# Turning Wk at the sixth tile, summing two biases on GpSimd, and spreading the reading of the expert weights

## The chip, the cores and the metric

The kernel runs on one core of a Trainium2 chip. The metric is the device time of one execution in microseconds. A core has a matrix engine (TensorE, "PE" in the profile, its weight loads "PEld"), three engines for elementwise work (VectorE "DVE", ScalarE "ACT", GpSimd "POOL"), a queue processor (SyncE, "SP") and 16 DMA engines. The engines run side by side, each works off its own list in order, and they wait for one another through semaphores.

## What is computed

A layer-normalised input of 2 x 1024 tokens of width 512 goes through attention (one head of width 512) and, beside it, through a mixture of 8 experts of which each token uses two. The second result gates the first:

```python
x = L0_attn_hidden_states
xn = _layernorm(x, axis=-1)
s = _L0_attn_ref(xn, w_qkv, b_qkv, w_out, b_out)
g = _silu(_L0_ffn_ref(xn, router_w, router_b, expert_w, expert_b, proj_w, proj_b, norm_w))
x = x + s * g
```

In attention `q, k, v = split(xn @ w_qkv.T + b_qkv)`, the scores are `q @ k.T / sqrt(512)`, softmax over keys, then `context @ w_out.T + b_out`. In the experts part, the logits `xn @ router_w + router_b` choose two experts with softmax weights; each expert is `silu(xn @ expert_w[e] + expert_b[e])`; the mix is projected, added to `xn`, and RMS-normalised.

## The kernel before

Everything is float32. The tokens are 16 tiles of 128 (`NT`), eight for each batch.

**Folded weights.** The kernel does not form q, k and v. It multiplies Wv with Wout once (`product_vo`, into `rwvo`), so that a tile's value rows come out of one product already in output form, and Wq with Wk (`product`, into `wqk`). Biases are folded too. `weighted(w_, bias, name)` forms a sum over four 128-row pieces of a weight, each multiplied by a column of bias: one multiplication, then three multiply-and-adds, four VectorE operations of 128 x 512. `columns` then sums over partitions with four one-column products against `ones`. Three such sums exist. `sq` (from Wq and bk) gives one extra router column `pw` that is stored in `rw[:, :, E]`, so that every tile's product over `rwvo` needs it. `sk` (from Wk and bq) gives `pu`, copied into `u`, the bias of the queries. `vb` (from Wout and bv) is summed over partitions by the product `pvb` and added to the output bias `bo`.

**Turned weights.** `wZ[0]` (Wq) and `wZ[1]` (Wk) come in by DMA and are transposed by `turn_w`: four VectorE transpositions of 128 x 512 into `wqkT`. All four must be done before any 128-row piece of `wqkT` is whole.

**The head.** GpSimd's list starts with constants and its share of the loads. VectorE takes statistics (`parts`), `means` and `variances` finish them with one small product each (`pmean`, `pvar`), ScalarE takes the root with `ln_eps` as its bias and normalises (`norm`), VectorE transposes the tile (`turn_x`), and SP writes the normalised tile to DRAM (`store`). Tiles 0 and 1 are done ahead of the loop.

**The tile loop** (line 500), t = 2 to 15. Step t transposes tile t+1 on VectorE, multiplies tile t by `rwvo` on TensorE (`value_half`, two halves with four products each, into `pv`), copies tile t-1 out of PSUM on ScalarE (`keep_values`) and normalises tile t+2. Statistics are closed for four tiles at a time, at t = 2, 5 and 9, by `means` between the halves and `variances` after them. Single pieces of other work hang on chosen steps: the turning of Wk at t = 8, `sk` at 9, `vb` at 10, `pu` at 11, `pvb` at 12, and the reads of all expert weights at 13 (32 DMAs of 256 KB, half issued by SP and half by GpSimd).

**After the loop** come the routing on VectorE, beside the products `pqk` and `pq`, then 39 expert slots (gather by GpSimd, two passes through DRAM for a transposition, four products of 512 columns each), then attention and the final gate.

**Order.** `keep_order` makes each engine keep the order in which the source issues its work. Temporary memory comes from pools: the `raw` pool holds the incoming weights and the three sums. The expert weights' tile `ew` takes that memory after `close(raw_guard)`, so its reads wait until the last readers of `raw` are done.

Of the kernel before, what the change touches and what calls it, by code (L numbers as in the profile page):

```python
# [10 lines left out]
FP = mybir.dt.float32  # L11
# [3 lines left out]
ALU = mybir.AluOpType  # L15
# [5 lines left out]
P = 128  # L21
LN_EPS = 1e-5
RMS_EPS = 1e-6
# [4 lines left out]
def kernel(  # L28
# [17 lines left out]
    B, S, H = hidden.shape  # L46
    E = router_w.shape[1]
    KC = H // P
# [13 lines left out]
    const = ctx.enter_context(tc.tile_pool(name="const", bufs=1))  # L62
    keep = ctx.enter_context(tc.tile_pool(name="keep", bufs=1))
    dram = ctx.enter_context(tc.tile_pool(name="dram", bufs=1, space=DRAM))
    ps_mm = ctx.enter_context(tc.tile_pool(name="ps_mm", bufs=4, space=PSUM))

    def pool(name, bufs=1, side="left", **where):
        guard = tc.tile_pool(name=name, bufs=bufs, side=side, reuse_waits="tile", **where)
        return guard, guard.__enter__()
# [3 lines left out]
    def close(guard):  # L73
        guard.__exit__(None, None, None)
# [25 lines left out]
    pe, dve, act, gps, sp = nc.tensor, nc.vector, nc.scalar, nc.gpsimd, nc.sync  # L100
# [8 lines left out]
    QP = P // 4  # L109
# [16 lines left out]
    def spread(eng, z, rows, quarters=range(4)):  # L126
        for q in quarters:
            eng.dma_start(
                z[ts(q, QP)], rows[:, ts(q, P)].rearrange("(i a) f -> a i f", a=QP)
            )  # L130

    def turn_w(dst, z):

        for r in range(KC):
            dve.transpose(
                dst.rearrange("p j (i q a) -> p i j q a", i=4, q=4)[:, :, :, r, :],
                z[:, ts(r, 4), :].rearrange("p i (j b) -> p i j b", b=QP),
            )
# [18 lines left out]
    wqkT = qT.rearrange("p k c f -> p (k c f)").rearrange("p (n f) -> p n f", f=H)  # L157
# [3 lines left out]
    raw_guard, raw = pool("raw", side="right")  # L161
# [6 lines left out]
    rw = rwvo[:, :, HH : HH + E1]  # L168
# [5 lines left out]
    def load_x(eng, quarters, t, n):  # L174
        for q in quarters:
            eng.dma_start(
                x[ts(q, QP), ds(t, n)].rearrange("p t i f -> p (t i) f"),
                xr_d[ds(t * P, n * P), ts(q, P)].rearrange("(n a) f -> a n f", a=QP),
            )

    wv_in = raw.tile([P, KC, H], FP, name="wv_in")
    wZ = [raw.tile([P, H // QP, P], FP, tag=f"wZ{i}", name=f"wZ{i}") for i in range(2)]
    wo = raw.tile([P, KC, H], FP, name="wo")
    bqkv = const.tile([P, 3, KC], FP, name="bqkv")
    bqk = const.tile([P, 2, KC], FP, name="bqk")
# [14 lines left out]
    ours, others = (0, 1), (2, 3)  # L200
# [28 lines left out]
    for q in range(4):  # L229
        for j in range(KC):  # L230
            gps.tensor_copy(bqk[ts(q, QP), :, j], bqkv[ts(j, QP), 0:2, q])  # L231
    spread(gps, wZ[0], w_qkvT[:, ts(0, H)], others)
    load_x(gps, others, 2, 2)
    for q in range(4):
# [1 line left out]
            rw[ts(q, QP), :, 0:E], router_w[ts(q, P), :].rearrange("(j b) e -> b j e", b=QP)  # L236
        )
    load_x(gps, others, 4, 4)
    ln_eps = const.tile([P, 1], FP, name="ln_eps")
    gps.memset(ln_eps, LN_EPS)  # L240
    rms_eps = const.tile([P, 1], FP, name="rms_eps")
    gps.memset(rms_eps, RMS_EPS)
    order = rc.tile([P, E], FP, name="order")
    for e in range(E):
        gps.memset(order[:, e : e + 1], float(E - e))
    ones = const.tile([P, P], FP, name="ones")
    gps.memset(ones, 1.0)

    rb = const.tile([P, E1], FP, name="rb")
    gps.dma_start(rb[:, 0:E], router_b.partition_broadcast(P))  # L250
    bo = const.tile([P, H], FP, name="bo")
# [15 lines left out]
    u = const.tile([P, KC], FP, name="u")  # L267
# [49 lines left out]

    def weighted(w_, bias, name):  # L320

        s_ = raw.tile([P, H], FP, tag="s", name=name, bufs=3)
        for c in range(KC):
            b_ = bias[:, c : c + 1]
            if c:
                dve.scalar_tensor_tensor(s_, w_[:, c, :], b_, s_, ALU.mult, ALU.add)
            else:
                dve.tensor_scalar(s_, w_[:, c, :], b_, None, ALU.mult)
            yield s_

    def columns(s_, name):

        ps = ps_mm.tile([P, 512], FP, tag="mm", name=name)
        for c in range(KC):
            pe.matmul(
                ps[:, c : c + 1], lhsT=s_[:, ts(c, P)], rhs=ones[:, 0:1], start=True, stop=True
            )
        return ps[:, 0:KC]

    def parts(t):  # L340
        for i in range(4):
            dve.bn_stats(st[:, t, i].rearrange("p h k -> p (h k)"), x[:, t, i, :])

    def across(a, name):

        ps = ps_mm.tile([P, 512], FP, tag="mm", name=name)
        n = a.shape[1] * 2
        pe.matmul(
            ps[:, :n], lhsT=eighth, rhs=a.rearrange("p m h -> p (m h)"), start=True, stop=True
        )  # L350
        return ps[:, :n].rearrange("p (m h) -> p m h", h=2)

    def means(t, n):
        g_ = ds(4 * t, 4 * n)
        at_ = st.rearrange("p t i h k -> p (t i) h k")[:, g_]
        dve.tensor_reduce(mean[:, g_], across(at_[:, :, :, 1], f"pmean{t}"), AX.X, ALU.add)
        dve.tensor_tensor(
            dev[:, g_],
            at_[:, :, :, 1],
            mean[:, g_].unsqueeze(2).to_broadcast([P, 4 * n, 2]),  # L360
            ALU.subtract,
        )
        dve.tensor_tensor(dev[:, g_], dev[:, g_], dev[:, g_], ALU.mult)
        dve.scalar_tensor_tensor(
            dev[:, g_], at_[:, :, :, 2], 8.0 / H, dev[:, g_], ALU.mult, ALU.add
        )
# [26 lines left out]
    def turn_x(t):  # L393
        turn(xnT[t // ST][:, :, ts(t % ST, P)], x[:, t], "(i a)")
# [49 lines left out]
    bb = raw.tile([P, KC], FP, name="bb")  # L444
# [2 lines left out]
    parts(2)  # L447
    parts(3)
    product_vo(1, 3)
    sum_q = weighted(wqkT[:, 0:KC], bqk[:, 1], "sq")  # L450
    next(sum_q)
    next(sum_q)


    pvs = {}
# [1 line left out]
    def value_half(t, n):  # L457
        if t not in pvs:
            pvs[t] = ps_big.tile([P, 2, 512], FP, tag="big", name=f"pv{t}")
        cols = (ds(0, HH + E1), ds(HH + E1, HH))[n]  # L460
        for c in range(KC):
            pe.matmul(  # L462
                pvs[t][:, n, : HH + E1 * (1 - n)],
                lhsT=xnT[t // ST][:, c, ts(t % ST, P)],
                rhs=rwvo[:, c, cols],
                start=(c == 0),
                stop=(c == KC - 1),
            )
# [5 lines left out]
        act.copy(lg1[:, t, :], pv[:, 0, HH : HH + E1])  # L474

    value_half(0, 1)
    means(2, 2)
    next(sum_q)
    sq_ = next(sum_q)
    value_half(1, 1)  # L480
    variances(2, 2)
    norm(2)
    norm(3)
    pbb = ps_mm.tile([P, 512], FP, tag="mm", name="pbb")
    pe.matmul(pbb[:, 0:KC], lhsT=ones, rhs=bb, start=True, stop=True)
    dve.tensor_reduce(rb[:, E:E1], pbb[:, 0:KC], AX.X, ALU.add)
    dve.tensor_copy(rw[:, :, E], columns(sq_, "pw"))
    value_half(0, 0)
    turn_x(2)
    keep_values(0)  # L490
# [9 lines left out]
    for t in range(2, NT):  # L500
        if 2 < t < NT - 1:
            turn_x(t + 1)
        value_half(t, 1)
        keep_values(t - 1)
        if t in (2, 5, 9):
            first = {2: 4, 5: 8, 9: 12}[t]
            means(first, 4)
        value_half(t, 0)
        if t in (2, 5, 9):
            variances(first, 4)  # L510
        if t + 2 < NT:
            norm(t + 2)
            if t % 2:
                store(t + 1)
        if 3 <= t < 7:
            parts(2 * t + 2)
            parts(2 * t + 3)
        if t == 2:
            gps.dma_start(bo, b_out.partition_broadcast(P))
        if t == 8:  # L520
            turn_w(wqkT[:, KC:], wZ[1])
        if t == 9:
            *_, sk_ = weighted(wqkT[:, KC:], bqk[:, 0], "sk")
        if t == 10:

            *_, vb = weighted(wo, bqkv[:, 2], "vb")
        if t == 11:
            dve.tensor_copy(u, columns(sk_, "pu"))
        if t == 12:
            pvb = ps_mm.tile([P, 512], FP, tag="mm", name="pvb")  # L530
            pe.matmul(pvb, lhsT=ones, rhs=vb, start=True, stop=True)  # L531
            dve.tensor_tensor(bo, pvb, bo, ALU.add)
            close(raw_guard)
        if t == 13:
            ew_guard, ewp = pool("ew", side="right")
            ew = ewp.tile([P, E, KC, H], FP, name="ew")
            for e in range(E):
                for q in range(4):
                    (sp if q in ours else gps).dma_start(  # L539
                        ew[ts(q, QP), e],  # L540
                        expert_w[e, ts(q, P), :].rearrange("(j b) f -> b j f", b=QP),
                    )
    keep_values(NT - 1)
    dve.tensor_tensor(lg1, lg1, rb.unsqueeze(1).to_broadcast([P, NT, E1]), ALU.add)
    close(ln_guard)
# [107 lines left out]
    first = rt.tile([P, E], FP, name="first")  # L653
# [48 lines left out]
    for g in range(2 * NT // LG):  # L702
# [7 lines left out]
        for j in range(LG):  # L710
# [3 lines left out]
                lhsT=lsel[:, j, :],  # L714
                rhs=tsel[:, i].rearrange("p k s -> p (k s)"),
                start=(i == 0),
                stop=(i == 2 * NT - 1),
# [40 lines left out]
    pw = pwp.tile([P, KC, H], FP, name="pw")  # L758
# [604 lines left out]
```

## Time and profile before

| what | value |
|---|---|
| three runs | 538.69, 541.28, 543.67 us; median 541.28 |
| the profiled execution | 540.82 us, its span 539.1 us |
| mean granted clock of TensorE | 0.995 |
| DMA | 112.37 MB, 208 GB/s over the span |
| VectorE's `sk`, its first operation and the three others | start 68.21 us, 0.48 and 2.33 us |
| VectorE's `vb`, the same | start 71.59 us, 0.44 and 2.33 us |
| GpSimd between its read of `bo` and its first read of `ew` | idle for 51.17 us |
| first and last issue of `ew` by SP, then `eb` | from 84.72 us, over 26.03 us; 111.78 us |

A row of the timeline gives a start in microseconds, a duration, engine, line and operation, the tile written and the tiles read; in brackets stands how long the engine was idle before it and what ended that. A row of groups gives the busy sum in us, the mean of one in ns, and the idle time before. Float32 products appear as two records each, so four products make eight. The digits of the slices are tenths of the busy share in 40 equal pieces of the span. A row of windows gives the stretch, its length, busy time with the number of instructions, the granted clock of TensorE, the DMA share and the bandwidth.

### The profile page before, as it was taken

To read this page: it belongs to the slowest core of one execution; us is meant where nothing else is said; L and a number is where in the kernel's file an instruction comes from. 1 tells how busy PE (TensorE), PEld (TensorE's weight loads), DVE (VectorE), ACT (ScalarE), POOL (GpSimd) and SP (SyncE) were. 2 spreads that over 40 slices of the span, in tenths; PEclk is the share of its full clock that TensorE was granted. 3 is DMA by queue.
4 is the path that set the end of the run, shared out by engine and by line. 5 is a ranking of instruction groups with operands and counts; after the bars stand their busy time and mean duration, and the time that the engine had idled before them with its cause. 6 is when DMAs were issued, how large, how long until landed. Compare 5 with 4: busy or idle time off the path is not lost.

```text
span 539.1 us, 5950 instructions
## 1 busy us (share of the span) xinstructions
PE 527.3 (98%) x1762; PEld 322.1 (60%) x1762; DVE 311.2 (58%) x565; ACT 167.0 (31%) x316; POOL 236.0 (44%) x272
## 2 busy tenths in 40 slices
PE   7999999999999999999999999999999999999996
PEld 5778877444444444444466656756846657484585
DVE  2565652840333333333859376375697685949586
ACT  1535562211311111111333422423426234152340
POOL 8610006022234875230227445246189755464542
PEclk9989999999999999999999999999999999999999
DMA  9995339999999999994387922723625638295512
GB/s 212 206 220 127 78 79 227 275 217 336 319 338 331 359 348 338 318 290 146 125 281 234 299 83 92 273 78 123 229 78 179 230 95 297 71 312 176 187 54 78
DMA packets 89057, 112.37 MB, mean 208 GB/s; under 512 B 6849, under 2 KB 59201, under 8 KB 88897
## 3 DMA queue, kind: packets, MB, share of 16 engines
q1 hardware_dynamic: 75072, 75.51, 47.5%
q0 software_dynamic: 8192, 26.24, 16.4%
q10 hardware_dynamic: 5760, 10.23, 5.0%
q8 instruction: 15, 0.25, 0.2%
q14 instruction: 18, 0.14, 0.1%
HBM read 70.54 MB, written 41.42 MB: 208 GB/s over the span
## 4 chain that ended last, share of the span: by engine, by line
PE 87%; DVE 6%; issue 3%; DMA 2%; POOL 1%; ACT 1%; DVEq 0%; POOLq 0%
PE ph L814 20%; PE so L1147 17%; PE pp L1076 14%; PE po L1013 10%; PE pv L462 10%; PE pq L555 5%; PE pr L574 4%; PE sc L1057 3%; PE pqk L586 3%; DMA wZ<-in_L_attn_w_qkv_dram 2%; DVE sc L1082 1%; DVE pT L120 1%; ACT x L380 1%; POOL bqk L231 1%; DVE h L840 1%
## 5 line engine op out<-in xcount | busy, mean ns | idle before, releaser
L814 PE MATMUL ph<-ew,gT 128*128 x280 | 120.3, 592 | 0.0
L814 PEld LDWEIGHTS ph<-ew,gT 128*128 128x128 f32 x280 | 53.2, 190 | 66.9 <-issue 66.9
L788 POOL DMA_INDIRECT xg<-xn_d,tok x39 | 37.3, 957 | 78.2 <-DMA xs<-xg 52.2
L840 DVE TENSOR_TENSOR h<-ph,eb 128x512 f32<-128x512 f32 x39 | 26.8, 690 | 75.6 <-issue 40.4
L462 PE MATMUL pv<-rwvo,xnT 128*128 128x256 f32 (+1 forms) x256 | 60.9, 394 | 1.8 <-DVE xnT L120 1.0
L462 PEld LDWEIGHTS pv<-rwvo,xnT 128*128 128x128 f32 x256 | 48.6, 194 | 11.2 <-ACT x L380 1.4
L843 ACT ACTIVATE h<-h 128x512 f32<-128x512 f32 x39 | 24.5, 629 | 97.7 <-DVE h L840 89.0
L1013 PE MATMUL po<-pw,ct 128*128 128x512 f32 x112 | 49.2, 592 | 0.0
L975 POOL DMA_INDIRECT hg<-ho_d,posi_m x32 | 32.4, 1013 | 37.0 <-DVE nm L1041 23.4
L1044 ACT ACTIVATE pr<-sc,nm 128x1024 f32<-128x1024 f32 x16 | 18.3, 1145 | 90.7 <-DVE nm L1041 89.0
L1154 DVE TENSOR_TENSOR o<-so,o 128x256 f32<-128x256 f32 x49 | 20.0, 421 | 38.8 <-PE so L1147 25.9
L1192 POOL TENSOR_TENSOR o<-o,base 128x512 f32<-128x512 f32 x14 | 20.6, 1493 | 45.3 <-DVE o L1157 45.3
L1076 PE MATMUL pp<-xnT,qT 128*128 128x512 f32 x84 | 39.5, 592 | 0.0
L1147 PE MATMUL so<-vo,pT 128*128 128x256 f32 x168 | 38.5, 379 | 0.0
L1013 PEld LDWEIGHTS po<-pw,ct 128*128 128x128 f32 x112 | 21.3, 190 | 25.5 <-issue 25.3
L1147 PEld LDWEIGHTS so<-vo,pT 128*128 128x128 f32 x168 | 31.9, 190 | 7.3 <-issue 2.6
L120 DVE STREAM_TRANSPOSE gT<-sz 128x512 f32<-128x512 f32 x39 | 27.4, 702 | 13.4 <-DMA sz<-xs 13.4
L1082 DVE TENSOR_TENSOR sc<-pp,sc 128x512 f32<-128x512 f32 x49 | 31.6, 679 | 5.2 <-PE pp L1076 5.2
L539 POOL DMA_DIRECT2D ew<-in_L_ffn_expert_w_dram x16 | 8.7, 551 | 57.6 <-PE pvb L531 51.2
L574 PE MATMUL pr<-xnT,wqk 128*128 128x256 f32 x128 | 28.8, 381 | 0.9 <-DVE sc L1082 0.9
L120 DVE STREAM_TRANSPOSE pT<-pz 128x1024 f32<-128x1024 f32 x14 | 28.2, 2011 | 0.2 <-DMA pz<-ps 0.2
L574 PEld LDWEIGHTS pr<-xnT,wqk 128*128 128x128 f32 x128 | 24.2, 190 | 6.6 <-DVE sc L1082 2.2
(227 smaller groups left out, 819.9 us busy)
## 6 DMA issues: line engine op xcount, KB each, us to landing
xs<-xg SPq DMA_DIRECT2D x39, 256.0 KB, 4.7
sz<-xs SPq DMA_DIRECT2D x39, 256.0 KB, 4.6
ho_d<-h ACTq DMA_DIRECT2D x39, 256.0 KB, 4.7
ps<-pr SPq DMA_DIRECT2D x16, 512.0 KB, 3.3
pz<-ps SPq DMA_DIRECT2D x16, 512.0 KB, 5.7
xn_d<-x SPq DMA_DIRECT2D x32, 128.0 KB, 2.4
ew<-in_L_ffn_expert_w_dram POOLq DMA_DIRECT2D x16, 256.0 KB, 10.9
ew<-in_L_ffn_expert_w_dram SPq DMA_DIRECT2D x16, 256.0 KB, 13.6
```

What stands on the lines that cost most here:

```text
L120: dve.transpose(dst.rearrange(f"p j {order} -> p i j a", a=QP), z.rearrange("p i (j b) -> p i j b", b=QP),)
L462: pe.matmul(pvs[t][:, n, : HH + E1 * (1 - n)], lhsT=xnT[t // ST][:, c, ts(t % ST, P)], rhs=rwvo[:, c, cols], start=(c == 0), stop=(c == KC ...
L555: pe.matmul(ps[:, half, :], lhsT=wqk[:, c, ts(oc, P)], rhs=xnT[0][:, c, ts(half, 512)], start=(c == 0), stop=(c == KC - 1),)
L574: pe.matmul(ps[:, :PW], lhsT=wqk[:, c, ts(oc, P)], rhs=xnT[1][:, c, ts(k, PW)], start=(c == 0), stop=(c == KC - 1),)
L788: gps.indirect_dma_start(out=xg[s], out_offset=None, in_=xn_d, in_offset=bass.IndirectOffsetOnAxis(ap=tok[:, s : s + 1], axis=0),)
L814: pe.matmul(ph, lhsT=g_[:, c, :], rhs=ew[:, ds(r, 1), c, :].rearrange("p e f -> p (e f)"), start=(c == 0), stop=(c == KC - 1),)
L840: dve.tensor_tensor(h, ph, eb[:, ds(r, 1), :].rearrange("p e f -> p (e f)"), ALU.add)
L975: gps.indirect_dma_start(out=g_, out_offset=None, in_=ho_d, in_offset=bass.IndirectOffsetOnAxis(ap=posi_m[:, n, t : t + 1], axis=0),)
L1013: pe.matmul(po, lhsT=c_[:, c, :], rhs=pw[:, c, :], start=(c == 0), stop=(c == KC - 1))
L1076: pe.matmul(ps, lhsT=l_[:, c, :], rhs=r_[:, c, :], start=(c == 0), stop=(c == KH - 1))
L1082: dve.tensor_tensor(dst, ps, other, ALU.add)
L1147: pe.matmul(ps[:, :w_], lhsT=l_[:, c, :], rhs=r_[:, c, :], start=(c == 0), stop=(c == SK - 1),)
```

## The change

`ln_eps`, `rms_eps` and `ones` are filled by GpSimd ahead of its first weight load. `weighted` takes an engine. On VectorE it does what it did; on another engine, each multiply-and-add is a multiplication into a temporary `m_` (two of these exist) and an addition, seven operations in all. `sq` stays on VectorE but is done in one go ahead of the value products of tiles 0 and 1; the second half of tile 1, `means`, `pbb` and `pw` are reordered around it, and `pw` is copied before `variances`. `vb` goes to GpSimd at t = 2 and `pvb` to t = 4. Wk is turned at t = 5, `sk` follows on GpSimd, `pu` is at t = 8, where `raw` is closed. The reads of the experts go one expert a step, t = 8 to 15. The statistics of tiles 12 to 15 move from t = 5 and 6 to t = 6 and 7.

```diff
+    ln_eps = const.tile([P, 1], FP, name="ln_eps")
+    gps.memset(ln_eps, LN_EPS)
+    rms_eps = const.tile([P, 1], FP, name="rms_eps")
+    gps.memset(rms_eps, RMS_EPS)
+    ones = const.tile([P, P], FP, name="ones")
+    gps.memset(ones, 1.0)
     spread(gps, wZ[0], w_qkvT[:, ts(0, H)], others)
...
     load_x(gps, others, 4, 4)
-    ln_eps = const.tile([P, 1], FP, name="ln_eps")
-    gps.memset(ln_eps, LN_EPS)
-    rms_eps = const.tile([P, 1], FP, name="rms_eps")
-    gps.memset(rms_eps, RMS_EPS)
...
-    ones = const.tile([P, P], FP, name="ones")
-    gps.memset(ones, 1.0)
...
-    def weighted(w_, bias, name):
+    def weighted(w_, bias, name, eng):
         s_ = raw.tile([P, H], FP, tag="s", name=name, bufs=3)
         for c in range(KC):
             b_ = bias[:, c : c + 1]
             if c:
-                dve.scalar_tensor_tensor(s_, w_[:, c, :], b_, s_, ALU.mult, ALU.add)
+                if eng is dve:
+                    dve.scalar_tensor_tensor(s_, w_[:, c, :], b_, s_, ALU.mult, ALU.add)
+                else:
+                    m_ = raw.tile([P, H], FP, tag="m", name=f"{name}_m{c}", bufs=2)
+                    eng.tensor_scalar(m_, w_[:, c, :], b_, None, ALU.mult)
+                    eng.tensor_tensor(s_, s_, m_, ALU.add)
             else:
-                dve.tensor_scalar(s_, w_[:, c, :], b_, None, ALU.mult)
-            yield s_
+                eng.tensor_scalar(s_, w_[:, c, :], b_, None, ALU.mult)
+        return s_
...
-    sum_q = weighted(wqkT[:, 0:KC], bqk[:, 1], "sq")
-    next(sum_q)
-    next(sum_q)
+    sq_ = weighted(wqkT[:, 0:KC], bqk[:, 1], "sq", dve)
...
     value_half(0, 1)
+    value_half(1, 1)
     means(2, 2)
-    next(sum_q)
-    sq_ = next(sum_q)
-    value_half(1, 1)
+    pbb = ps_mm.tile([P, 512], FP, tag="mm", name="pbb")
+    pe.matmul(pbb[:, 0:KC], lhsT=ones, rhs=bb, start=True, stop=True)
+    dve.tensor_copy(rw[:, :, E], columns(sq_, "pw"))
     variances(2, 2)
     norm(2)
     norm(3)
-    pbb = ps_mm.tile([P, 512], FP, tag="mm", name="pbb")
-    pe.matmul(pbb[:, 0:KC], lhsT=ones, rhs=bb, start=True, stop=True)
     dve.tensor_reduce(rb[:, E:E1], pbb[:, 0:KC], AX.X, ALU.add)
-    dve.tensor_copy(rw[:, :, E], columns(sq_, "pw"))
...
-        if 3 <= t < 7:
-            parts(2 * t + 2)
-            parts(2 * t + 3)
+        if t in (3, 4, 6, 7):
+            first = {3: 8, 4: 10, 6: 12, 7: 14}[t]
+            parts(first)
+            parts(first + 1)
         if t == 2:
             gps.dma_start(bo, b_out.partition_broadcast(P))
-        if t == 8:
-            turn_w(wqkT[:, KC:], wZ[1])
-        if t == 9:
-            *_, sk_ = weighted(wqkT[:, KC:], bqk[:, 0], "sk")
-        if t == 10:
-            *_, vb = weighted(wo, bqkv[:, 2], "vb")
-        if t == 11:
-            dve.tensor_copy(u, columns(sk_, "pu"))
-        if t == 12:
+            vb = weighted(wo, bqkv[:, 2], "vb", gps)
+        if t == 4:
             pvb = ps_mm.tile([P, 512], FP, tag="mm", name="pvb")
             pe.matmul(pvb, lhsT=ones, rhs=vb, start=True, stop=True)
             dve.tensor_tensor(bo, pvb, bo, ALU.add)
+        if t == 5:
+            turn_w(wqkT[:, KC:], wZ[1])
+            sk_ = weighted(wqkT[:, KC:], bqk[:, 0], "sk", gps)
+        if t == 8:
+            dve.tensor_copy(u, columns(sk_, "pu"))
             close(raw_guard)
-        if t == 13:
             ew_guard, ewp = pool("ew", side="right")
             ew = ewp.tile([P, E, KC, H], FP, name="ew")
-            for e in range(E):
-                for q in range(4):
-                    (sp if q in ours else gps).dma_start(
...
+        if 0 <= t - 8 < E:
+            e = t - 8
+            for q in range(4):
+                (sp if q in ours else gps).dma_start(
```

More of the change, by code (lines that the diff above doesn't have):

```diff
@@ L532 @@
             dve.tensor_tensor(bo, pvb, bo, ALU.add)
+        if t == 5:
[3 more added lines that the diff above has]
+            dve.tensor_copy(u, columns(sk_, "pu"))
             close(raw_guard)
-        if t == 13:
             ew_guard, ewp = pool("ew", side="right")
             ew = ewp.tile([P, E, KC, H], FP, name="ew")
-            for e in range(E):
-                for q in range(4):
-                    (sp if q in ours else gps).dma_start(
-                        ew[ts(q, QP), e],
-                        expert_w[e, ts(q, P), :].rearrange("(j b) f -> b j f", b=QP),
-                    )
+        if 0 <= t - 8 < E:
+            e = t - 8
+            for q in range(4):
+                (sp if q in ours else gps).dma_start(
+                    ew[ts(q, QP), e],
+                    expert_w[e, ts(q, P), :].rearrange("(j b) f -> b j f", b=QP),
+                )
     keep_values(NT - 1)
```

## The prediction

> **What bounds the kernel now.** I read the page first (busy shares, slices), then the waits of TensorE, then the timeline of the first 92 us, and last the granted clock in single microseconds.
>
> ```profile
> PE 527.3 (98%) x1762; PEld 322.1 (60%) x1762; DVE 311.2 (58%) x565; ACT 167.0 (31%) x316; POOL 236.0 (44%) x272
> PE   7999999999999999999999999999999999999996
> PEclk9989999999999999999999999999999999999999
> ```
>
> TensorE is busy 98% of the span. Its idle time is about 12 us in all, most of it in the first 32 us and the last 5 us. So only two things can change the time: work taken off TensorE (the change takes none off, it only moves it) and TensorE's waits, old and new. Its waits before 130 us are:
>
> ```profile
> PE pvo L411 <- DMA wo<-in_L_attn_w_out_dram: 1.3, 1, 1.3
> PE hold L216 <- POOL idle L211: 1.2, 1, 1.2
> PE pv L462 <- DVE xnT L120: 1.0, 1, 1.0
> PE pw L335 <- DVE sq L326: 0.9, 1, 0.9
> ```
>
> The change can touch the last two. The timeline shows where they are:
>
> ```profile
> 30.69 1.05 PE L335 MATMUL pw<-ones,sq 128*128 128x1 f32 x8 [0.92 <-DVE sq L326]
> 32.00 4.34 PE L462 MATMUL pv<-rwvo,xnT 128*128 128x265 f32 x11 [0.26 <-DVE rwvo L487]
> ...
> 52.65 0.19 DVE L370 TENSOR_REDUCE var<-pvar 128x16 f32<-128x32 f32 x1 [1.13 <-PE pvar L348]
> ...
> 59.55 2.45 DVE L135 STREAM_TRANSPOSE qT<-wZ 128x512 f32<-128x512 f32 x4
> ...
> 68.72 2.33 DVE L326 SCALAR_TENSOR_TENSOR sk<-qT,bqk,sk 128x512 f32<-128x512 f32 x3
> ...
> 70.96 0.70 DVE L120 STREAM_TRANSPOSE xnT<-x 128x512 f32<-128x512 f32 x1
> ...
> 71.81 3.75 PE L462 MATMUL pv<-rwvo,xnT 128*128 128x256 f32 x16 [0.99 <-DVE xnT L120]
> ```
>
> At 71.81 TensorE has waited 0.99 us for tile 11, whose transposition stood behind the sum `sk` on VectorE. Each token tile holds TensorE about 3.6 us (the retained copies wait for tiles 7 and 8 to end at 59.85 and 63.36). VectorE needs 1.2 us from the end of `pvar` (52.45) to the last scale factor (53.67).
>
> **The change, part by part.** I follow times of this execution, and write what each part does to TensorE.
>
> 1. *The constants ahead of the weight loads.* `std` (20.31) waited 1.16 us for `ln_eps`; now it can start after its table load, at 19.15. But TensorE is filled by `pvo` until 24.57 whatever happens, and tile 0's transposition stands behind the weight turning, which waited for its own DMA until 21.85. TensorE's restart at 25.09 moves by at most 0.1 us. Against it, three memsets (0.25 us on GpSimd) stand ahead of the weight loads. Bounds -0.1 to +0.25; I take 0. The last two memsets matter to no one earlier.
>
> 2. *The whole `sq` sum ahead of the statistics.* Now VectorE does the four operations in a row (0.47 + 3 x 0.75 us, from 27.05), so `sq` ends near 29.95 instead of 30.65. `pw` (1.05 us) then ends near 31.05, the 0.16 us copy near 31.25, and tile 0's product starts near 31.4 instead of 32.00, with `pvar` now in front of it: about -0.55 us. The price is that tiles 2 and 3 are normalised 0.8 us later (tile 2 turned by 34.7 rather than 33.9). TensorE needs tile 2 only near 36.8, and the statistics of tiles 4 to 7 end near 38.4 where `pmean` asks near 38.5. That cover is thin, and I give 0.2 us of range to it.
>
> 3. *`vb` on GpSimd and `pvb` at t=4.* After its DMA issue GpSimd is idle from 29.96 to 81.13. Seven operations from 30 us are done near 40; TensorE asks near 48. Hidden with 8 us to spare. `pvb` itself (0.86 us on the chain) moves from t=12 to t=4: zero in sum, but it delays tiles 5 on until it is paid back. Its addition on VectorE (0.69 us) precedes tile 6's transposition, which still ends some 2 us before it is asked for.
>
> 4. *The turning of Wk at t=5.* The order on VectorE becomes: statistics of tiles 8 to 11, four transpositions (2.49 us at 21.85), tile 7's transposition, and only then the next statistics (1.64 us). Shift so far: -0.55 + 0.86 = +0.3 us, so `pvar` ends near 52.75, the factors are ready at 53.98, Wk at 56.45, tile 7 at 57.15; with 0.1 us of latency TensorE gets it at 57.25. It has been ready since 52.75 + 3.6 = 56.4: a new wait of 0.85 us.
>
> 5. *`sk` on GpSimd, used at t=8.* The sum cannot start before all four pieces of Wk are turned, 56.5. TensorE reaches `pu` after tiles 7 and 8: 57.25 + 7.2 = 64.45. So there are 8.0 us for seven operations. Queued behind `pu` on TensorE is everything. The rows for their cost:
>
> ```profile
> L859 POOL TENSOR_TENSOR vo<-vo,bo 128x512 f32<-128x512 f32 x16 | 20.4, 1277 | 0.3
> L299 POOL TENSOR_SCALAR mix<-mixed,number 128x128 f32<-128x128 f32 x1 | 0.6, 622 | 0.1
> L225 POOL TENSOR_SCALAR eighth<-eighth 128x32 f32<-128x32 f32 x1 | 0.3, 316 | 0.1
> ```
>
> Three additions cost 1.28 us each. The four multiplications by a column have no row at 512 elements. The two smaller rows, put on a line, give 0.62 + 384 x 3.2 ns = 1.85 us. The Trainium skill speaks for far less: its GPSIMD Engine Reference, section Engine selection, calls two-input work about twice as slow as on VectorE but one-input work roughly line-rate, which with a fixed 0.25 us and its 1.2 GHz is an estimate of 0.7 us. By the rule `sk` takes 4 x 0.7 + 3 x 1.28 + 0.5 (gaps of 0.08) = 7.1 us and is ready in time; by the line it takes 11.7 us and TensorE waits 3.8. The row at 128 elements is 0.62 us where the rule would give 0.36, so I do not follow the rule; nor do I believe the line, whose two points differ in operation and kind of operand. I take the addition's 1.28 us as the same size with one operand less: 9.4 us, ready near 66.1, a wait of 1.7 us (bounds 0 and 3.8).
>
> 6. *What VectorE is relieved of.* `sk` and `vb` (2.8 us each) leave it at t=9 and t=10. Tile 11 is then turned right after the factors, some 1.7 us before it is wanted: the 0.99 us wait goes (0.96 on the chain). `pu` (0.79 us) only moves.
>
> 7. *Expert weights from t=8.* They wait for `pu`, so from near 67 rather than 81 us; the SP queue issues two of them between the stores of each pair of tiles, GpSimd's the others behind `sk`. In the trace before, SP takes 26.0 us for its 16 (84.72 to 110.75) and `eb` follows at 111.78. All that earlier arrival is worth nothing: from 91 to 250 us TensorE waits for no transfer. The cost side: the stores of the last tiles now stand behind weights on SP, but the first gather asks for them at 115.24, over 20 us later. Zero, bounded at -0.2 to +0.3.
>
> Sum: -0.55 + 0.85 + 1.7 - 0.96 = +1.04 us. The profiled execution took 540.82 us (span 539.1), so 541.9. It lies 0.46 under the median of the three runs (541.28), whose spread is 5 us; I predict 542.0.
>
> **The clock.** After thin work TensorE was granted half speed:
>
> ```profile
> 29.00:32.00 3.00, 1.82 (x14) 0.98 1.14 213
> 32.00:35.00 3.00, 3.00 (x7) 0.50 1.08 243
> 70.00:72.00 2.00, 1.01 (x5) 1.00 0.84 200
> ```
>
> The columns are busy time, granted clock, DMA share, GB/s. About 1.2 us idle plus one-column products between 29 and 32 us were followed by some 3.4 us at 0.50: a loss of 1.7 us. A single wait of 0.99 us at 71 cost no clock. The Trainium skill (TensorE: Matmul & The Clock Gate, Part 1) makes the gate close after an idle window of about 3.4 us that runs free of the program; by that rule a wait of 1.7 us costs nothing more. Here it closed after less. With `pu` (one-column products) behind it, the new wait is like the stretch at 29 to 32, so I give one chance in three that it closes (+1.7), and leave it out of the likeliest case. Equally, the shorter gap at 30 us may spare the old closing (-1.7).
>
> **Rivals.**
> - *GpSimd is quick enough* (multiplications below 0.93 us, so `sk` within 8.0 us): no wait at `pu`, sum -0.66, 540.2 to 540.6. For it: the rule above, and nothing else on GpSimd then. Against: 0.62 us at 128 elements.
> - *GpSimd is the bound and the clock falls* (the slower side): multiplications of 1.85 us make the wait 3.8 us, which empties TensorE for longer than the gap at 30 us did, and half clock for 3.4 us costs 1.7: 1.04 + 2.1 + 1.7 = +4.9, 545.7 to 546.2. It decides from a wait of about 2 us on, thus from multiplications of about 1.4 us.
> - *The gate does not close at 32 us any more* and `sk` is in time: -0.66 - 1.7 = -2.4, about 538.5.
> That the weights' earlier reading wins is a rival without a place: no wait for them exists to remove.
>
> **Chances.** Likeliest case 0.50; quick GpSimd 0.20; slow GpSimd with the clock 0.20; no half clock 0.10. 1% is 5.4 us, about what a measurement can tell, and even the single runs before spread by nearly that. No case wins 1%; only spread below the third rival would: faster 0.05. Slower by 1% needs the slow case plus spread above the median or a second closing: 0.15. Same: 0.80. Range 539.0 to 546.0: from the quick case less a microsecond of spread to the slow one.
>
> **What would show it.** `pw` some 0.6 us earlier; a wait before tile 7's product of about 0.9 us released by the transposition; a wait before `pu` of 1 to 2 us released by GpSimd; no wait at tile 11; GpSimd's multiplications near 1.3 us. I am wrong if `pu` never waits, if the clock row shows 0.5 after it, or if TensorE shows waits past 92 us that were not there.

## The result and the profile after

The changed kernel takes 545.46 us (median of 18 runs, 540.91 to 547.39) against 540.22 us (538.69 to 543.67, 18 runs): a ratio of 1.0083 with a 95% interval of 1.006 to 1.0105. It is slower by a little less than 1% (5.2 us by the two medians, about 4.5 us by the ratio), where I had forecast +1.04 us. Run again later it gave 1.0100 (1.0076 to 1.0123). The profiled execution took 547.39 us (span 545.7), the longest of its 18 runs, so its 6.6 us over the profiled execution of before overstate the usual loss.

Busy shares and slices of the changed kernel:

```profile
PE 530.2 (97%) x1762; PEld 324.6 (59%) x1762; DVE 307.6 (56%) x557; ACT 167.1 (31%) x316; POOL 256.3 (47%) x286
...
PE   7979799999999999999999999999999999999996
...
PEclk9999979999999999999999999999999999999999
```

VectorE lost 3.6 us of work and GpSimd took on 20.3. The half-clock dip (the digit under 9 in the row `PEclk`) has left the third slice and sits in the sixth, deeper. TensorE's waits tell the rest:

```profile
PE pu L339 <- POOL sk L330: 2.4, 1, 2.4
PE pv L464 <- ACT lg L476: 1.9, 1, 1.9
...
PE pw L339 <- DVE sq L326: 1.3, 1, 1.3
...
PE pv L464 <- ACT x L384: 0.7, 1, 0.7
PE pmean L352 <- DVE st L346: 0.3, 1, 0.3
```

The wait for tile 11 is gone. In its place stand a wait for `sk` at `pu`, one at t = 2 and one at tile 7. The timeline around `pu`:

```profile
58.20 1.56 POOL L332 TENSOR_SCALAR sk<-qT,bqk 128x512 f32<-128x512 f32 x1 [18.59 <-DVE qT L135]
...
59.74 1.56 POOL L329 TENSOR_SCALAR sk_m<-qT,bqk 128x512 f32<-128x512 f32 x1
...
61.39 1.27 POOL L330 TENSOR_TENSOR sk<-sk,sk_m 128x512 f32<-128x512 f32 x1
...
67.17 1.26 POOL L330 TENSOR_TENSOR sk<-sk,sk_m 128x512 f32<-128x512 f32 x1
68.48 1.87 PE L339 MATMUL pu<-ones,sk 128*128 128x1 f32 x8 [2.37 <-POOL sk L330]
```

GpSimd begins as soon as Wk is turned and needs 10.2 us (58.20 to 68.43); TensorE has been idle since 66.11. And this is the clock there, in windows of TensorE (length, busy time, granted clock, DMA share, GB/s):

```profile
65.00:68.00 3.00, 1.11 (x5) 1.00 0.00 0
68.00:71.00 3.00, 2.52 (x10) 0.56 0.00 0
71.00:74.00 3.00, 3.00 (x9) 0.50 0.87 201
74.00:77.00 3.00, 3.00 (x14) 0.80 1.08 213
```

TensorE is granted half speed from 68.37 to 75.20 us, 6.8 us in all. From the start of `pu` to `pvar` of t = 9 the work takes 8.0 us (start of `pu` at 68.48 to `pvar` at 76.48, start to start) where the trace of before has 0.79 for `pu` and 3.56 for tile 9 up to the same mark (63.36 to 66.92): 3.65 us more, nearly all of it the clock (half of 6.83 us is 3.4). The mark, before and after:

```profile
66.92 0.30 PE L348 MATMUL pvar<-dev,eighth 128*128 128x32 f32 x2
...
76.48 0.30 PE L352 MATMUL pvar<-dev,eighth 128*128 128x32 f32 x2
```

The slow work shows as busy 3.00 in these windows, so without the clock column the larger half of what this execution loses at `pu` would look like ordinary work.

Lead and lag of the profiled execution against before, at marks of TensorE's timeline: first product of tile 0 after `pw`, 31.97 against 32.00 (0.0); `pvar` of t = 2, 42.12 against 41.04 (+1.1); `pvar` of t = 5, 54.24 against 52.31 (+1.9, of which 0.86 is `pvb`, only moved); tile 7, 58.84 against 56.1 (+2.7); `pvar` of t = 9, 76.48 against 66.92 (+9.6); `pqk`, 97.80 against 91.22 (+6.6). The lead of before shrinks between the last two marks because it still has `pu` (0.79), `pvb` (0.86) and its wait for tile 11 (0.99) ahead of it at 66.92. From `pqk` on nothing changes: the end is 6.6 later too. The whole loss lies in the tile loop.

### The profile page after: what moved, and what is told of

Same layout as the page of the kernel before. It is cut to its first block, busy times and chain, and to the rows that moved or that the text cites. A ratio compares the mean times of both kernels' runs of the same rounds, so it can differ in the third digit from the quotient of the medians.

```text
span 545.7 us, 5957 instructions
## 1 busy us (share of the span) xinstructions
PE 530.2 (97%) x1762; PEld 324.6 (59%) x1762; DVE 307.6 (56%) x557; ACT 167.1 (31%) x316; POOL 256.3 (47%) x286
## 4 chain that ended last, share of the span: by engine, by line
PE 84%; DVE 7%; DMA 3%; issue 3%; POOL 2%; SPq 1%; ACT 1%; DVEq 0%; POOLq 0%
PE ph L813 20%; PE so L1146 17%; PE pp L1075 14%; PE po L1012 10%; PE pv L464 7%; PE pq L554 5%; PE pr L573 4%; DMA wZ<-in_L_attn_w_qkv_dram 3%; PE sc L1056 3%; PE pqk L585 3%; DVE qT L135 1%; DVE st L346 1%; POOL sk_m L329 1%; DVE sc L1081 1%; DVE pT L120 1%
## 5 line engine op out<-in xcount | busy, mean ns | idle before, releaser
L1012 PEld LDWEIGHTS po<-pw,ct 128*128 128x128 f32 x112 | 21.3, 190 | 25.5 <-issue 25.3
L554 PE MATMUL pq<-xnT,wqk 128*128 128x512 f32 x64 | 28.1, 595 | 0.0
```

Source lines behind the costliest of these rows:

```text
L554: pe.matmul(ps[:, half, :], lhsT=wqk[:, c, ts(oc, P)], rhs=xnT[0][:, c, ts(half, 512)], start=(c == 0), stop=(c == KC - 1),)
L1012: pe.matmul(po, lhsT=c_[:, c, :], rhs=pw[:, c, :], start=(c == 0), stop=(c == KC - 1))
```

## The experiments

My theory A: the time goes at `pu`, as a wait for GpSimd and as half clock behind it. Rivals: B, GpSimd's `vb` slows VectorE in the head; C, the earlier reading of expert weights costs. All versions start from the changed kernel but one. The kernel before was run beside each group; its medians were 540.04, 540.17 and 539.48 us in the three groups, so ratios are compared.

**pu one tile later**

```diff
-        if t == 8:
+        if t == 9:
             dve.tensor_copy(u, columns(sk_, "pu"))
```

> The changed kernel with pu, the end of the raw pool and the first expert's read one tile later (t = 9; the last step reads two experts). Theory A (the time goes at pu: 2.37 us of waiting for sk and then 3.65 us at half clock, in the profiled run): sk is ready near 68.4 us, tile 9 ends near 70, so no wait and no half clock; 539.5 to 541 us, ratio 0.998 to 1.002. Theory B (the time goes in the head, where GpSimd's vb takes the SBUF reads from VectorE): nothing changes, 544.5 to 546. Theory C (reading the expert weights from t = 8 is what costs): little changes, 544 to 546.

The end of `raw` and the reading of the first expert move along with it. Measured 539.17 us, ratio 0.9994 (0.9978 to 1.0009). In its timeline `pu` starts at 68.23 without waiting, the clock column stays at 1.00, and the waits at t = 2 (1.1 us) and tile 7 (0.71) are still there. The whole loss is gone. B can't explain that, since `vb` is where it was; C could only by the one step by which the reading moved, and that is tested below.

**sk back on VectorE, pu left where the change put it**

```diff
+        if t == 7:
+            sk_ = weighted(wqkT[:, KC:], bqk[:, 0], "sk", dve)
...
-            sk_ = weighted(wqkT[:, KC:], bqk[:, 0], "sk", gps)
```

> The changed kernel with only sk put back on VectorE, at t = 7 behind tile 8's transposition; pu stays at t = 8 and the experts' reads where the change put them. Theory A in its narrow form (it is GpSimd's 10.2 us for the sum, not the place of pu): sk takes 2.8 us and is ready near 62.5 us, no wait at pu, no half clock there, ratio 0.998 to 1.001 as with pu at t = 9. If VectorE becomes the bound instead: a wait of 1 us or more at tile 9's transposition, and 1.002 to 1.005. Theory B alone: no change, 1.007 to 1.010.

Measured 540.01 us, ratio 1.0002 (0.9986 to 1.0019). Its VectorE timeline:

```profile
57.65 0.69 DVE L120 STREAM_TRANSPOSE xnT<-x 128x512 f32<-128x512 f32 x1
58.27 0.44 DVE L332 TENSOR_SCALAR sk<-qT,bqk 128x512 f32<-128x512 f32 x1
58.74 2.33 DVE L326 SCALAR_TENSOR_TENSOR sk<-qT,bqk,sk 128x512 f32<-128x512 f32 x3
60.99 1.64 DVE L346 BATCH_NORM_STATS2 st<-x 128x6 f32<-128x128 f32 x8
```

The sum ends at 61.1, and `pu` begins at 63.46 as soon as tile 8 is done. So it is not the early place of `pu` that costs but GpSimd's 10.2 us for a sum that VectorE does in 2.8, between tile 8's transposition and the next statistics, where it had room.

**Fillers in front of pu: the clock apart from the wait**

```diff
         if t == 8:
+            hold(16)
             dve.tensor_copy(u, columns(sk_, "pu"))
```

> The changed kernel with 16 filler products (bf16, 256 columns, about 0.14 us each, result unused) on TensorE in front of pu. Theory A with the clock as the larger half: the wait of 2.37 us is still spent (the fillers stand in it), but TensorE does not go idle and the clock stays at 1.00 after pu, so about 3.6 us of the loss go away: 541 to 542.5 us, ratio 1.002 to 1.005. If the wait alone were the loss and the half clock had another cause: 545 to 546, with 0.5 in the clock column near 70 us all the same. Theories B and C: no change, 544.5 to 546.

> The changed kernel with 22 filler products in front of pu instead of 16, so that they end about when sk is ready and no idle time is left there (16 left 0.63 us). Theory A with the half clock as a loss of its own: clock 1.00 after pu in the profile, 1.5 to 3.5 us below the unaltered changed kernel of this call, though the 2.4 us stay spent. If the clock falls because of tile 8's place or of the one-column products alone, it falls here too and the time does not differ by more than 1 us.

> The changed kernel unaltered, on the same chip as the three others of this call, as their yardstick. All theories: ratio 1.006 to 1.0105, a wait of about 2.4 us before pu; how often the clock falls behind it is what its runs are to tell.

The second version has `hold(22)`. With 16 fillers: 543.77 us, ratio 1.0066 (1.0042 to 1.0089), short of the 3.6 us that I expected; the intervals of this and the unaltered kernel's 1.0083 overlap. In its profile `pu` still waits 0.63 us behind the fillers, and the clock holds:

```profile
67.00:70.00 3.00, 2.50 (x15) 1.00 0.09 23
```

In the last group the unaltered changed kernel gave 544.35 us, 1.0100 (1.0076 to 1.0123), and 22 fillers gave 542.71 us, 1.0057 (1.0036 to 1.0078): 2.3 us less by the ratios, though those intervals still touch. The timeline and the windows of the version with 22:

```profile
65.31 2.56 PE L216 MATMUL hold<-idle 128*128 128x256 bf16 x22
67.86 1.05 PE L339 MATMUL pu<-ones,sk 128*128 128x1 f32 x8
```

```profile
65.00:68.00 3.00, 3.00 (x27) 1.00 0.00 0
68.00:71.00 3.00, 3.00 (x19) 1.00 0.35 102
```

The time to `pu` is spent as before, and the clock holds. In the unaltered kernel of that group the wait was 2.39 us and the clock fell:

```profile
65.00:68.00 3.00, 2.17 (x11) 0.77 0.00 0
68.00:71.00 3.00, 3.00 (x12) 0.66 0.94 250
```

Here the half clock cost 3 x (0.23 + 0.34) = 1.7 us, half of what it cost in the first profile.

What it costs on the mean can be read from the runs themselves. Each is recorded with its mean granted clock, and one minus that, times the span, is the time lost to half clock (an estimate, to about 0.3 us for a single run):

| runs | lost to half clock, mean | span without it, mean |
|---|---|---|
| kernel before, 107 runs in the three groups | 1.65 us | 536.6 us |
| changed kernel, 24 runs | 3.0 us | 540.1 us |
| with fillers, 16 runs | 1.5 us | 540.2 us |
| `pu` at t = 9, 14 runs | 0.9 us | 536.9 us |

The standard errors are 0.1 us in the first row and 0.3 to 0.4 us in the others. So of a mean loss of 4.8 us the half clock is 1.4 and waiting 3.4; the fillers take away the first and leave the second, and one tile of room takes away both. Of the 3.4 us, the traces show 2.4 at `pu`; where the last microsecond goes stays open.

**When the clock falls.** A wait alone does not lower it. In the profile of the changed kernel TensorE also waited 1.85 us at t = 2, and the clock stayed at 1.00. The clock's record in the traces tells the two apart. In all 14 traces the times between one change of the clock and the next, while the kernel runs, are whole multiples of 3.413 us (27.31, 61.44 and 471.04 us are 8, 18 and 138 of them). So I lay windows of that length through each trace from the clock's first rise, and count in each only the products of more than 32 columns, which leaves out `pw`, `pu`, `pmean` and `pvar` (that line is drawn to fit; in the tile loop every product has 32 columns or fewer, or 256 or more). For the changed kernel (rise at 6.93 us), these are four windows with the products `pv` alone, the only such products there:

```profile
34.24:37.65 3.41, 1.57 (x8) 1.00 1.05 220
...
64.96:68.37 3.41, 1.15 (x6) 1.00 0.00 0
68.37:71.79 3.42, 1.58 (x4) 0.50 0.07 11
71.79:75.20 3.41, 3.33 (x9) 0.50 1.06 242
```

The first, with 1.57 us of them, kept the clock; after the second, with 1.15, it fell. The third was not enough to bring it back, the fourth was: hence two windows of half clock instead of one. Over the 2133 windows at full clock before 530 us in all 14 traces there is no exception: the clock fell after each of the nine with up to 1.40 us (a share of 0.41), and after none with 1.57 us (0.46) or more. At half clock it came back after every window with a share of 0.92 or more. By this a wait counts no more than the one-column products behind it; together they make a hole of 3.3 us at `pu`, and where the windows' edges fall in it is chance. If the dividing share is 0.41 to 0.46, an edge spares the clock in 11 to 21% of executions (an estimate); 4 of the 24 runs have a mean clock of 0.999 or 1.000. With 16 fillers the window at `pu` is filled to 0.55, and the clock holds.

**vb held back**

```diff
-            vb = weighted(wo, bqkv[:, 2], "vb", gps)
-        if t == 4:
+        if t == 3:
+            bv = raw.tile([P, KC], FP, name="bv")
+            dve.tensor_copy(bv, bqkv[:, 2])
+            vb = weighted(wo, bv, "vb", gps)
+        if t == 7:
             pvb = ps_mm.tile([P, 512], FP, tag="mm", name="pvb")
```

> The changed kernel with vb held back: its bias column goes through a small copy on VectorE in step 3, and pvb moves to t = 7. Theory B: VectorE's sums sq take 0.75 us again in place of 0.91, the scale factor of tiles 2 and 3 0.17 in place of 0.95, tile 0's product starts near 31.4 us and the waits at t = 2 (1.85 and 0.34 us) go, so 2 to 3 us less than the changed kernel: 542 to 543.5. Theory A: the wait before pu stays 2 to 3.5 us (sk can't start earlier than Wk's turning, which comes earlier by what the head gains), so the time stays above 542. If the head's loss is not from GpSimd, 544.5 to 546.

> pu at t = 9 as in the first experiment, and vb held back as in the third (pvb at t = 7). Theory B in its own right (GpSimd's vb in the head costs about 1 us beside the wait at pu): 1 us or more below the first experiment's ratio of 0.9994, so 0.996 to 0.998. If the third experiment only gained because pvb, moved to t = 7, gave sk 0.86 us more time before pu: no difference from the first, 0.9985 to 1.0005.

Alone: 542.5 us, 1.0044 (1.0025 to 1.0063), as theory B wanted. But it moves `pvb` in front of `pu`, which gives `sk` 0.86 us more; the wait at `pu` was 1.87 us and the half clock behind it cost 1.7 us. The waits at t = 2, which theory B had go, stayed: 0.93 and 0.34 us. With `pu` at t = 9 the confusion is removed: 538.8 us, 0.9983 (0.9971 to 0.9994) against 0.9994 without the holding back. The intervals overlap: B's share is 0.6 us by these ratios and not told apart from nothing (with Wk turned later, below, holding back gives 0.9976 against 0.9968, the other way). The way in which it can cost, though, is plain in one timeline of the changed kernel:

```profile
30.92 1.56 POOL L329 TENSOR_SCALAR vb_m<-wo,bqkv 128x512 f32<-128x512 f32 x1
...
31.16 0.47 DVE L368 SCALAR_TENSOR_TENSOR dev<-st,dev 128x16 f32<-128x16 f32 x1
...
32.56 1.26 POOL L330 TENSOR_TENSOR vb<-vb,vb_m 128x512 f32<-128x512 f32 x1
...
32.90 0.95 DVE L377 SCALAR_TENSOR_TENSOR shift<-mean,rstd 128x8 f32<-128x8 f32 x1
...
33.89 2.42 ACT L384 ACTIVATE x<-x,shift,rstd 128x128 f32<-128x128 f32 x6 [1.26 <-DVE shift L377]
```

The operation `shift` on eight columns, 0.17 us in the trace before, takes 0.95 us and ends when GpSimd's addition does (33.82). ScalarE waits for it, tile 2 is normalised late, and so is everything on ScalarE's list, among it the copy of tile 0's values that TensorE waits for at 37.66. The Trainium skill (SBUF — State Buffer, section Who interferes with whom) says that a VectorE instruction with two SBUF inputs contends with a GpSimd instruction that reads SBUF, and calls the port pair that they share an exclusive lock. For the addition the trace agrees. For the multiplication it agrees only in part: the row `dev` at 31.16 takes 0.47 us instead of 0.17 and ends 0.7 us into a multiplication of 1.56 us (GpSimd's spans are rough), and with `pu` at t = 9 such a row of 0.18 us (30.57) lies wholly inside one.

What meets what is chance. With `vb` held back `shift` takes 0.17 us, but it does so too with `vb` in its place, in the profile with `pu` at t = 9 and in that of the changed kernel run again; the wait for ScalarE's copy at t = 2 is then 1.11 and 0.93 us, against 0.93 with `vb` held back. So the first profile shows about 0.9 us of B, and the others 0 to 0.2.

**Expert weights read as before, at t = 13**

```diff
-        if 0 <= t - 8 < E:
-            e = t - 8
+        for e in range(E) if t == 13 else []:
```

> The changed kernel with all 32 reads of expert weights at t = 13, as before. Theories A and B: no change beyond 0.5 us, 544.5 to 546, ratio 1.007 to 1.011. Theory C: 540.5 to 542.

545.73 us, 1.0099 (1.007 to 1.0128). The wait at `pu` is again 2.37 us. Theory C falls: when the weights are read makes no difference that these runs can show.

**The head of the change alone, on the kernel before**

```diff
-    next(sum_q)
-    next(sum_q)
+    *_, sq_ = sum_q
     value_half(0, 1)
+    value_half(1, 1)
     means(2, 2)
...
+    dve.tensor_copy(rw[:, :, E], columns(sq_, "pw"))
     variances(2, 2)
```

(with `pbb` ahead of `pw`, and the constants ahead of the weight loads, as in the change)

> The kernel before with only the head of the change: the constants first, sq in one go, tile 1's second half and pw ahead, pvar after. GpSimd has no sum to do. The prediction's step (-0.55 us): tile 0's product 0.5 to 0.7 us sooner after sq's start than before, no new wait at t = 2, ratio 0.998 to 1.000. If the later normalisation of tiles 2 and 3 costs at t = 2 even without GpSimd: a wait of about 1 us released by ScalarE's copies, which eats the gain, ratio 1.000 to 1.002.

539.39 us, 0.9983 (0.997 to 0.9995): about 0.9 us gained, a little more than the step's 0.55. From the first product of tile 0 (24.88) to its second half (31.41) there are 6.53 us, 6.91 in the trace before. There was no wait at t = 2. But the half clock was there, between 32 and 35 us, as in the trace before. In each of the five of the 14 traces that have it there, TensorE waits at most 0.2 us at t = 2; in each of the nine without it, TensorE arrives sooner and waits there 1.3 to 2.2 us for ScalarE's copy, for statistics or for both. The slow clock and the wait cover the same 1.5 us or so.

**Versions meant to beat both**

```diff
+        if t == 6:
+            turn_w(wqkT[:, KC:], wZ[1])
+            sk_ = weighted(wqkT[:, KC:], bqk[:, 0], "sk", gps)
         if t in (3, 4, 6, 7):
...
-        if t == 5:
-            turn_w(wqkT[:, KC:], wZ[1])
-            sk_ = weighted(wqkT[:, KC:], bqk[:, 0], "sk", gps)
-        if t == 8:
+        if t == 10:
```

> The changed kernel with Wk turned at t = 6, behind tile 7's transposition and ahead of the statistics of tiles 12 and 13, and pu at t = 10. Theory A, with the wait at tile 7 as the part of its own that the first experiment left (0.71 us): no wait of more than 0.2 us at tile 7, at pu or at tile 11; 0.7 us below the first experiment, ratio 0.9975 to 0.999. If turning Wk there delays tile 8 instead, a wait released by a transposition near 60 us and no gain.

> Wk turned at t = 6, pu at t = 10 and vb held back to step 3 with pvb at t = 7; the order of ScalarE's copies as in the changed kernel. Theory B on top of A: 0.3 to 0.8 us below the version with the late turning alone (ratio 0.9968), so 0.995 to 0.9965, 537.2 to 538 us. If vb's place costs nothing: the same as that version, 0.996 to 0.998.

> All together: Wk turned at t = 6, pu at t = 10, vb held back, and ScalarE copies tile 0's values out between the normalisations of tiles 2 and 3 instead of after both. The waits at t = 2 (1.1 to 1.9 us), tile 7 (0.7), pu and tile 11 all go: 536.5 to 538.5 us, ratio 0.993 to 0.997. If the copy in front only delays tile 3, a wait released by a transposition near 38 us and 538 to 539.5.

The late turning with `pu` at t = 10: 538.18 us, 0.9968 (0.9954 to 0.9983). With `vb` held back too: 538.15 us, 0.9976 (0.9962 to 0.999). With tile 0's copy moved in front of tile 3's normalisation as well: 538.3 us, 0.9977 (0.9965 to 0.999). All three beat the kernel before by 1.2 to 1.7 us and the changed kernel by about 6; among themselves they can't be told apart. In the first, tile 8 waits 0.40 us for its transposition, as I had feared, and tile 7 no longer. In the second, TensorE waits nowhere between 40 and 90 us; I had expected 0.995 to 0.9965 of it, for a share of B that did not show. The third only moved a wait. Its waits of TensorE:

```profile
PE pmean L352 <- DVE st L346: 1.5, 1, 1.5
```

The copy no longer holds tile 2, but the statistics of tiles 4 to 7 still end at 36.4, and `pmean` waits for those. My expectation that the waits at t = 2 would go was wrong: two engines had the same lateness.

## Why the prediction came out as it did

The range held the time. The likeliest case had the right waits (tile 7, `sk` at `pu`, none at tile 11) and too small a size: +1.04 us against about +4.5 by the ratio. That lies near the rival "GpSimd is the bound and the clock falls" (+4.9), in part by luck: the rival put 3.8 us on the wait at `pu`, which took 2.37, and it had no wait at t = 2. Of the signs named ahead, one that I am wrong came true: the clock row shows 0.5 after `pu`. The wait there is above 1 to 2 us, GpSimd's multiplications are above 1.3, and `pw` is no earlier (30.66 against 30.69).

- *Step 1, the constants:* right. `std` started at 19.79, and tile 0's product in the head did not gain (25.31 against 25.09).
- *Step 2, sq in one go:* right for the head by itself (the head alone gained 0.9 us), but none of it arrived in the changed profile. `sq` ended at 30.6 rather than 29.95, its last operation taking 1.01 us beside GpSimd's first multiplication, in place of 0.75. The cover that I called thin was indeed none: 1.85 us of wait for ScalarE's copy and 0.34 for `pmean`. The old half clock at 32 us was spared, as one of my rivals had it, though behind a longer gap (1.31 us) and not a shorter one; the wait at t = 2 took what that gained. I had looked at tile 2's transposition and the statistics, and not at that copy, which stands behind both normalisations on ScalarE's list.
- *Step 3, vb hidden with 8 us to spare:* right that TensorE never waits for `pvb`; wrong that the work is free wherever it falls, since I asked only who waits for its result and not whom it keeps from working (about 0.9 us in one profile, next to nothing in others).
- *Step 4, the wait at tile 7:* forecast 0.85, measured 0.70.
- *Step 5, sk:* the mis-sized term. The multiplication takes 1.56 us, not 1.28, between my value and the line through the small rows (1.85). Four of them add 1.1 us, and gaps smaller than I allowed give 0.3 back: 10.2 us in place of 9.4. TensorE waited 2.37 us in place of 1.7.
- *The clock,* the largest term left out: I gave one chance in three that it falls. It fell in each of the four profiles in which `pu` waited with nothing in front of it (1.87 to 2.39 us), for 3.4 us in three and 6.8 in one, and over the runs it is worth about 1.4 us more than before. The prediction set the wait alone against an idle window of 3.4 us. The traces show windows of that length, but one need not be empty: a share of 0.41 of wide products is too little, and the one-column products of `pu` do not count. With the 1.7 us that I forecast and 0.8 for `pu`, the same estimate as above makes the clock fall in 55 to 65% of executions. It belonged in the likeliest case: 1.04 + 1.7 = +2.7.
- *Step 6:* right, tile 11 does not wait. *Step 7:* right, zero.

## What to carry to other kernels

When a sum moves from VectorE to GpSimd, size it at GpSimd's rate from its start to the moment its reader asks; here 2.8 us became 10.2, against 8 us of room, and one more tile of room (3.6 us) was all that was lacking. On a kernel that TensorE bounds, a wait of about two microseconds with thin products behind it is priced with the half clock that may follow, and the clock column is read before a slow stretch is called work. An engine that "has nothing to do" may still hold up a tiny operation on the critical chain (0.95 us in place of 0.17 here).

## What the hardware showed unexpectedly

- GpSimd's multiplication by a column (128 x 512, one tensor read) takes 1.56 us, longer than its addition of two tensors of the same size (1.27 us). The rule in the prediction, that one-input work runs near line rate, does not hold for it.
- TensorE's clock fell after each 3.41 us window that products of more than 32 columns filled to 0.41 or less, and after none filled to 0.46 or more, in 14 traces. One-column products count as little as waiting: TensorE was busy for up to 0.79 of a window after which the clock fell, and a wait of 1.85 us between wide products left it at 1.00. The half clock lasts one window (3.4 us, a loss of 1.7), or two where the next one is thin as well.
- The first 25 us differ from execution to execution: in the profiles taken, tile 0's product started between 23.4 and 25.3 us, which may be part of why single runs of one kernel spread by 3 to 6 us. Three runs of versions with `pu` at t = 8 were long at a mean clock of 0.999 (547.15 and 546.32 us of the changed kernel, 545.0 with 16 fillers); the cause was not found, since no trace of them exists.
